# A recurrent layer times a routed expert layer: routed rows that carry their weight, and a new order of the units

## Chip, cores and metric

The kernel runs on one core of one Trainium2 chip. The metric is the device time of one execution in microseconds (us). Five engines work beside each other, each through its own queue in order: PE (matrix multiplies; PEld is its weight loads), DVE and ACT (elementwise work; ACT also evaluates the nonlinear functions), POOL (elementwise work, and it issues indirect DMAs) and SP (issues DMAs). They wait for one another by semaphores.

## What is computed

All data are float32: x is 4 x 1024 tokens of 256 channels. It is normalised (xn), and two branches are computed from xn:

```python
# branch 1: recurrence
xt = layernorm(xn) * ln_w + ln_b;  xp = xt shifted by one token
K, V = mix(xt, xp, mk) @ Wk.T, mix(xt, xp, mv) @ Wv.T
R = sigmoid(mix(xt, xp, mr) @ Wr.T)
S[t] = S[t-1] * decay + K[t]
s = xn + (R * (S * first + K) * V) @ Wo.T
# branch 2: experts, 8 of 128 hidden channels, the best 2 of the better group of 4
w = the two chosen sigmoid scores / their sum
f = sum over the 2 chosen e: w[e] * ((silu(xn @ w_gate[e]) * (xn @ w_up[e])) @ w_down[e])
f += (silu(xn @ sw_gate) * (xn @ sw_up)) @ sw_down      # shared expert
out = x + s * silu(f)
```

## The kernel before

**Groups.** The tokens are 8 groups g of 512 (two to a batch row b), each held as 4 tiles of 128 tokens. `norm` (moments on DVE, a square root on ACT at L311, a DVE product at L322) makes xn from x, `turn_xn` transposes it on PE, and ACT copies the result out. `norm2`, `norm2_out` and `turn_xt` do the same for the second norm. `diff` (POOL, L370) and `mix` (DVE, L645) make the mixed inputs. `gate` (L660), `recur` (L673 to L677), `value` (L682 on DVE, L683 on POOL) and `project_out` (L691 on PE, L694 on DVE, which overwrites xn) are the recurrence.

**Shared expert.** `shared_in` multiplies with the weights held on PE and 512 tokens moving, so that its result `hs` is already turned. `shared_out` multiplies down and ACT copies it to `acc` (L717).

**Routing.** `scores` computes router logits (64 small matmuls in all, L384) and their sigmoid (L388). `choose` picks the experts on DVE for a batch row, `place` computes each token's row in a list by expert and scatters it there with 16 indirect DMAs on POOL (L492); the list `xs` lies in DRAM. `plan`, once per half of the batch (two rows), starts with a matmul `cnt` (L506) and a DVE comparison `more` (L515), and derives which expert each tile of 128 list rows has; it ends with zero rows written behind each expert's list (L555).

**Expert tiles.** Each half has 39 tiles, worked on in 20 pairs: `tile_load` (SP, L589, three `xe` buffers), `tile_turn` (four transposes a pair, L597, copied by ACT, L599), `tile_in` (`gu`, L607, silu L611, product L612), `tile_back` (transposes L619, ACT copy L621), `tile_out` (`ye`, L628, ACT copy L630, then SP writes to `ys`, L632).

**Combining.** `fetch` gathers the two expert rows of 128 tokens with two indirect DMAs on POOL (L737), into six buffers. `combine` adds them on DVE, times their weights, to `acc` (L748). `final` applies silu on ACT (L757), multiplies by s and adds x on DVE (L758, L759) and writes out (SP, L760).

**Order.** The list ORDER (L25 to L117) is written out by hand or by a planner and holds every unit. PE, DVE and ACT execute in exactly this order; the chains of `follow` (L197) order the queues of SP and POOL. Tiles with a `bufs` count are recycled, so an instruction that writes such a tile waits for the last reader of the one before.

## Time and profile before

| What | Value |
|---|---|
| median of 8 runs | 417.92 us (413.98 to 420.27) |
| the profiled execution's own time | 421.44 us |
| its span (first to last instruction) | 419.7 us |
| busy PE / PEld / DVE / ACT / POOL | 345.1 / 241.3 / 253.7 / 195.0 / 171.3 us |
| mean granted clock of TensorE | 0.925 |
| 78 `xe` loads, 78 `ys` writes | 128 KB each |
| DMA | 58.96 MB, mean 140 GB/s |

A group line reads: line, engine, operation, output <- inputs, shape, count | busy us, mean ns of one | idle time of the engine just before, and what ended it. A line of a timeline reads: start us, duration us, engine, line, operation, output <- inputs, count [idle before <- what ended it]. A line of a table of stretches reads: from:to, its length, the busy time (and instructions) of PE, PEld, DVE, ACT and POOL, the granted clock, the DMA share and GB/s. Busy times of overlapping instructions are counted once in a total.

### The profile page before, as it was taken

Reading aid. Unit: us, or ns where it says so; the run is one execution under the profiler, and the core shown is the slowest. Engines: PE = TensorE matmul, PEld = TensorE weight load, DVE = VectorE, ACT = ScalarE, POOL = GpSimd, SP = SyncE. Lnnn points to the kernel's source line nnn. Section 1 sums busy time; section 2 is a strip of 40 time slices with the busy share of each in tenths; the row PEclk is TensorE's granted clock in tenths of the full one; section 3 lists DMA queues with packets and bytes.
Section 4 is the critical chain, followed back from the end, with each engine's and each line's share of the span. In section 5 each row is a group of like instructions: output and inputs, shape, how many; then the busy total and the mean of one; then the engine's idle time right before and its main releaser. Section 6 shows DMA issues by size and latency. Waiting matters only on the chain.

```text
span 419.7 us, 5291 instructions
## 1 busy us (share of the span) xinstructions
PE 345.1 (82%) x1426; PEld 241.3 (57%) x1426; DVE 253.7 (60%) x642; ACT 195.0 (46%) x347; POOL 171.3 (41%) x190
## 2 busy tenths in 40 slices
PE   1999957986899899539689998998679999977950
PEld 1756434662488687336248886787357856526430
DVE  4679984823934373434531544944348879689686
ACT  1874463453477654053156795153186443432501
POOL 7101576472010026727620131567610234768760
PEclk9999985989899899859969999999989999998986
DMA  7984141121544326215262564358655343516544
GB/s 223 308 266 145 55 152 44 52 100 50 164 138 149 104 79 215 109 60 167 100 210 67 184 181 125 99 162 231 197 159 177 106 142 108 152 37 187 150 124 139
DMA packets 52748, 58.96 MB, mean 140 GB/s; under 512 B 6800, under 2 KB 48272, under 8 KB 52720
## 3 DMA queue, kind: packets, MB, share of 16 engines
q1 hardware_dynamic: 45552, 40.39, 30.7%
q0 software_dynamic: 6608, 18.23, 13.4%
q8 instruction: 12, 0.20, 0.2%
q14 instruction: 16, 0.13, 0.1%
q10 hardware_dynamic: 560, 0.02, 0.1%
HBM read 31.61 MB, written 27.00 MB: 140 GB/s over the span
## 4 chain that ended last, share of the span: by engine, by line
PE 42%; DVE 19%; another core or an unknown queue 9%; DMA 8%; issue 8%; ACT 7%; SPq 3%; POOL 2%; ACTq 0%; DVEq 0%; POOLq 0%
PE gu L607 11%; PE ye L628 6%; PE r L653 5%; PE y L691 4%; DVE mix L645 3%; PE v L653 3%; PE tre L597 3%; PE k L653 3%; DVE acc L748 3%; DMA xe<-xs 2%; DVE S L673 2%; PE trh L619 2%; PE sh L703 2%; DMA got<-ys,back 2%
## 5 line engine op out<-in xcount | busy, mean ns | idle before, releaser
L492 POOL DMA_INDIRECT xs<-xn,idx x64 | 62.7, 980 | 43.0 <-DVE den L483 24.8
L737 POOL DMA_INDIRECT got<-ys,back x64 | 64.0, 999 | 39.3 <-issue 14.3
L607 PE MATMUL gu<-wgu,xeT 128*128 x312 | 75.5, 385 | 0.0
L607 PEld LDWEIGHTS gu<-wgu,xeT 128*128 128x128 f32 x312 | 58.1, 194 | 8.6 <-issue 1.7
L683 POOL TENSOR_TENSOR A<-A,rs 128x512 f32<-128x512 f32 x16 | 21.9, 1377 | 99.6 <-DVE A L682 96.5
L612 DVE TENSOR_TENSOR act<-act,gu 128x256 f32<-128x256 f32 (+1 forms) x40 | 16.5, 412 | 70.8 <-ACT act L611 64.1
L628 PE MATMUL ye<-wd,hT 128*128 x156 | 41.9, 394 | 0.0
L748 DVE SCALAR_TENSOR_TENSOR acc<-got,wt,acc 128x256 f32<-128x256 f32 x64 | 32.3, 512 | 13.9 <-DMA got<-ys,back 12.2
L645 DVE SCALAR_TENSOR_TENSOR mix<-d,vec,xtT 128x512 f32<-128x512 f32 x48 | 38.2, 842 | 0.0
L630 ACT COPY yes<-ye 128x512 f32<-128x512 f32 (+1 forms) x40 | 23.0, 577 | 32.7 <-PE ye L628 13.7
L370 POOL TENSOR_TENSOR d<-xtT 128x1024 f32<-128x1024 f32 x8 | 15.3, 1916 | 54.2 <-ACT xtT L362 25.6
L597 PE MATMUL tre<-ident,xe 128*128 128x128 f32 x156 | 26.0, 280 | 13.3 <-ACT hT L621 5.3
L691 PE MATMUL y<-wo,A 128*128 128x256 f32 x128 | 31.8, 398 | 4.5 <-POOL A L683 4.5
L703 PE MATMUL sh<-xnT,wgus 128*128 128x512 f32 x64 | 34.1, 688 | 0.0
L611 ACT ACTIVATE act<-gu 128x256 f32<-128x256 f32 (+1 forms) x40 | 15.2, 380 | 40.2 <-PE gu L607 22.3
L628 PEld LDWEIGHTS ye<-wd,hT 128*128 128x128 f32 x156 | 29.3, 200 | 5.5 <-issue 2.2
L653 PE MATMUL r<-mix,wr 128*128 128x512 f32 x64 | 31.3, 636 | 0.0
L597 PEld LDWEIGHTS tre<-ident,xe 128*128 128x128 f32 x156 | 19.2, 143 | 20.9 <-issue 7.7
L653 PE MATMUL k<-mix,wk 128*128 128x512 f32 x64 | 31.1, 614 | 0.0
L599 ACT COPY xeT<-tre 128x512 f32<-128x512 f32 (+1 forms) x40 | 23.0, 576 | 16.1 <-PE tre L597 8.7
L691 PEld LDWEIGHTS y<-wo,A 128*128 128x128 f32 x128 | 24.9, 201 | 9.5 <-POOL A L683 6.2
L653 PE MATMUL v<-mix,wv 128*128 128x512 f32 x64 | 29.7, 594 | 0.6 <-DVE A L677 0.6
(127 smaller groups left out, 536.8 us busy)
## 6 DMA issues: line engine op xcount, KB each, us to landing
xe<-xs SPq DMA_DIRECT2D x78, 128.0 KB
ys<-yes SPq DMA_DIRECT2D x78, 128.0 KB
xs<-zeros SPq DMA_DIRECT2D x32, 128.0 KB
xf<-in_x SPq DMA_DIRECT2D x16, 256.0 KB
out<-acc SPq DMA_DIRECT2D x16, 256.0 KB
xg<-in_x SPq DMA_DIRECT2D x7, 512.0 KB
wgu<-in_w_gate SPq DMA_DIRECT2D x8, 128.0 KB
wgu<-in_w_up SPq DMA_DIRECT2D x8, 128.0 KB
```

Of the source, the lines that this page charges most:

```text
L492: put = nc.gpsimd.indirect_dma_start(out=xs[h][:, :], out_offset=bass.IndirectOffsetOnAxis(ap=idx[:, k, n : n + 1], axis=0), in_=xn[:, n % ...
L597: nc.tensor.transpose(tr[:, c, j, :], p["xe"][:, j, ts(c, P)], ident)
L599: nc.scalar.copy(p["xeT"][:, :, :n], tr[:, :, :n])
L607: nc.tensor.matmul(gu[:, j, :], p["xeT"][:, c, j, :], wgu[:, e, c, :], start=(c == 0), stop=(c == CC - 1))
L628: nc.tensor.matmul(y[:, j, :], p["hT"][:, j, :], wd[:, e, :], start=True, stop=True)
L630: nc.scalar.copy(ye[:, :n], y[:, :n])
L645: nc.vector.scalar_tensor_tensor(m[:, c, :], d[:, c, :], vec[:, c, which : which + 1], xtT[:, c, 0:G], ALU.mult, ALU.add)
L653: nc.tensor.matmul(ps, w[:, c, ts(dc, P)], src[:, c, :], start=(c == 0), stop=(c == CC - 1))
L691: nc.tensor.matmul(ps[:, j, :], A[:, c, ts(2 * h + j, P)], wo[:, c, :], start=(c == 0), stop=(c == CC - 1))
L703: nc.tensor.matmul(p, wgu_s[:, c, ts(i, I)], xnT[:, c, :], start=(c == 0), stop=(c == CC - 1))
L737: follow(nc.gpsimd.indirect_dma_start(out=got[:, :], out_offset=None, in_=ys[b // BPH][:, :], in_offset=bass.IndirectOffsetOnAxis(ap=route ...
L748: nc.vector.scalar_tensor_tensor(acc, parts.pop((g, i, k)), route_of[b]["wt"][:, k, n : n + 1], acc, ALU.mult, ALU.add)
```

## The change

- x is loaded straight into the tile that keeps xn, and `norm` works in place; each token row there is 264 columns wide (W), 8 more than before. `norm` and `norm2` treat one, two or four groups at once.
- A routed row carries its weight in column 256. Since a token has two weights, ACT makes a second copy of its rows (`copy_rows`); POOL clears the extra columns. `place` writes the weights into the rows, and the scatters send 264 columns.
- `tile_out` scales its result by the weight while copying from PSUM, one ACT instruction per tile instead of one per pair; it reads the weight from `xe`. There are four `xe` buffers instead of three.
- `fetch` gathers with addition straight into `acc`, four tiles of one choice k at a time; `combine` is gone.
- The router's 8 columns are joined to the shared expert's weights. `shared_in` now holds 128 tokens and moves 264 weight columns; `scores` is gone, ACT copies the logits out and `choose` applies the sigmoid. `shared_turn` transposes the result.
- The gate uses tanh(z/2): `value` multiplies by (tanh + 1) and `project_out` by 0.5. A has two buffers.
- ORDER is new as a whole: more of the shared expert and all norms stand ahead of the expert tiles, and less is left behind them.

```diff
--- before.py
+++ after.py
@@ ORDER (whole list replaced; its beginning, the end of its tile stage and its end) @@
+    ("norm", 0, 1), ("turn_xn", 0, 0), ("turn_xn", 0, 1), ("norm2", 0, 1), ("norm2_out", 0), ("norm", 1, 1),
+    ("shared_in", 0, 0), ("load_x", 4), ("shared_in", 0, 1), ("turn_xn", 1, 0), ("turn_xn", 1, 1),
+    ("shared_turn", 0), ("turn_xt", 0, 0), ("turn_xt", 0, 1), ("shared_out", 0, 0), ("norm", 2, 2),
+    ("shared_in", 1, 0), ("load_x", 5), ("shared_in", 1, 1), ("turn_xn", 2, 0), ("load_x", 6), ("load_x", 7),
+    ("diff", 0), ("turn_xn", 2, 1), ("mix", 0, 2), ("choose", 0), ("shared_out", 0, 1), ("turn_xn", 3, 0),
+    ("shared_turn", 1), ("shared_in", 2, 0), ("turn_xn", 3, 1), ("shared_in", 2, 1), ("copy_rows", 1),
+    ("shared_out", 1, 0), ("copy_rows", 0), ("shared_out", 1, 1), ("place", 0), ("shared_turn", 2), ("gate", 0),
+    ("norm2", 1, 1), ("norm2_out", 1), ("shared_out", 2, 0), ("shared_out", 2, 1), ("turn_xt", 1, 0),
+    ("turn_xt", 1, 1), ("norm", 4, 4), ("shared_in", 3, 0), ("shared_in", 3, 1), ("turn_xn", 4, 0),
+    ("turn_xn", 4, 1), ("choose", 1), ("turn_xn", 5, 0), ("copy_rows", 3), ("turn_xn", 5, 1), ("copy_rows", 2),
+    ("shared_turn", 3), ("shared_in", 4, 0), ("shared_out", 3, 0), ("shared_in", 4, 1), ("shared_out", 3, 1),
+    ("place", 1), ("shared_turn", 4), ("turn_xn", 6, 0), ("plan", 0), ("shared_out", 4, 0), ("turn_xn", 6, 1),
...
+    ("tile_out", 1, 19), ("fetch", 4, 0), ("gate", 6), ("final", 1, 0), ("fetch", 4, 1), ("shared_out", 6, 0),
+    ("mix", 7, 2), ("project_out", 4, 0), ("final_load", 4, 1), ("fetch", 5, 0), ("project_out", 4, 1),
+    ("recur", 6, 0), ("final", 4, 0), ("shared_out", 6, 1), ("shared_turn", 7), ("final_load", 5, 0),
...
+    ("final_load", 6, 0), ("fetch", 7, 0), ("gate", 7), ("recur", 7, 0), ("recur", 7, 1), ("project_out", 6, 1),
+    ("value", 7, 1), ("final", 6, 1), ("value", 7, 0), ("project_out", 6, 0), ("final_load", 7, 0), ("final", 6, 0),
+    ("fetch", 7, 1), ("final_load", 7, 1), ("project_out", 7, 1), ("project_out", 7, 0), ("final", 7, 0),
+    ("final", 7, 1),
...
+    W = C + 8
...
-    xs = [dram.tile([NROW, C], F32, tag=f"xs{h}", name=f"xs{h}") for h in range(NH)]
+    xs = [dram.tile([NROW, W], F32, tag=f"xs{h}", name=f"xs{h}") for h in range(NH)]
...
-        xg = tok.tile([P, NT, C], F32, tag="xg", name=f"xg_{g}", bufs=3)
+        xg = keep.tile([P, NT, W], F32, tag=f"xn{g}", name=f"xn_{g}")
+        state[g]["row0"] = xg
+        xg = xg[:, :, 0:C]
...
+    wgu_s = wts.tile([P, CC, 2 * I + E], F32, tag="wgus", name="wgus")
...
+    nc.scalar.dma_start(wgu_s[:, :, 2 * I :], routerT.rearrange("(c p) e -> p c e", p=P))
...
+    def norm(g, many):
+
+        mv, rstd = moments(range(g, g + many), 1)
+        for n in range(many * NT):
+            xn = state[g + n // NT]["xn"][:, n % NT, :]
+            nc.vector.tensor_scalar(xn, xn, mv[:, n, 0:1], rstd[:, n : n + 1], ALU.subtract, ALU.mult)
+
+    def copy_rows(g):
+
+        row = tok.tile([P, NT, W], F32, tag="row1", name=f"row1_{g}", bufs=2)
+        for r in (row, state[g]["row0"]):
+            follow(nc.gpsimd.memset(r[:, :, C:], 0.0))
+        nc.scalar.copy(row[:, :, 0:C], state[g]["xn"])
+        state[g]["row1"] = row
+
+    def norm2(g, many):
+
+        n_all = many * NT
+        mv, rstd = moments(range(g, g + many), 2)
+        off = small.tile([P, 4 * NT], F32, tag="off", name=f"off_{g}", bufs=2)
+        nc.vector.scalar_tensor_tensor(off[:, :n_all], mv[:, :n_all, 0], -1.0, rstd[:, :n_all], ALU.mult, ALU.mult)
+        for i in range(many):
+            state[g + i]["norm2"] = off[:, ts(i, NT)], rstd[:, ts(i, NT)]
 
...
-    def scores(b, hb):
-        if hb == 0:
-            scores_of[b] = small.tile([P, BT, E], F32, tag="sc", name=f"sc_{b}", bufs=2)
-        xnT = state[b * GPB + hb]["xnT"]
-        lg = ps_tr.tile([P, G], F32, tag="tr", name=f"lg_{b}_{hb}")
-        for n in range(NT):
-            for c in range(CC):
-                nc.tensor.matmul(
-                    lg[:, ts(n, E)], xnT[:, c, ts(n, P)], rw[:, c, :], start=(c == 0), stop=(c == CC - 1)
-                )
-        sc = scores_of[b][:, ts(hb, NT), :]
-        nc.scalar.activation(sc.rearrange("p n e -> p (n e)"), lg[:, : NT * E], AF.Sigmoid)
-
     def choose(b):
 
         sc = scores_of[b]
+        flat = sc.rearrange("p n e -> p (n e)")
+        nc.scalar.activation(flat, flat, AF.Sigmoid)
 
...
-        wt = keep.tile([P, K, BT], F32, tag=f"wt{b}", name=f"wt_{b}")
-        tt(wt, w, den.unsqueeze(1).to_broadcast([P, K, BT]), ALU.mult)
-        route_of[b].update(wt=wt, row=got[:, 0, :])
+        for i in range(GPB):
+            for k in range(K):
+                tt(state[b * GPB + i][f"row{k}"][:, :, C], w[:, k, ts(i, NT)], den[:, ts(i, NT)], ALU.mult)
+        route_of[b].update(row=got[:, 0, :])
 
         for n in range(BT):
-            xn = state[b * GPB + n // NT]["xn"]
             for k in range(K):
                 put = nc.gpsimd.indirect_dma_start(
                     out=xs[h][:, :], out_offset=bass.IndirectOffsetOnAxis(ap=idx[:, k, n : n + 1], axis=0),
-                    in_=xn[:, n % NT, :], in_offset=None,
+                    in_=state[b * GPB + n // NT][f"row{k}"][:, n % NT, :], in_offset=None,
                 )
...
-        xe = exp.tile([P, 2, C], F32, tag="xe", name=f"xe_{h}_{u}", bufs=3)
+        xe = exp.tile([P, 2, W], F32, tag="xe", name=f"xe_{h}_{u}", bufs=4)
...
-        nc.scalar.copy(ye[:, :n], y[:, :n])
+        for j in range(n):
+            nc.scalar.activation(ye[:, j, :], y[:, j, :], AF.Copy, scale=p["xe"][:, j, C : C + 1])
...
-            nc.scalar.activation(r[:, dc, :], ps[dc], AF.Sigmoid)
+            nc.scalar.activation(r[:, dc, :], ps[dc], AF.Tanh, scale=0.5)
...
-            st["A"] = chan.tile([P, CC, G], F32, tag="A", name=f"A_{g}", bufs=1)
+            st["A"] = chan.tile([P, CC, G], F32, tag="A", name=f"A_{g}", bufs=2)
...
-        tt(A, A, v_ps, ALU.mult)
-        follow(nc.gpsimd.tensor_tensor(A, A, state[g]["r"][:, dc, :], ALU.mult))
+        rv = state[g]["r"][:, dc, :]
+        nc.vector.scalar_tensor_tensor(rv, rv, 1.0, v_ps, ALU.add, ALU.mult)
+        follow(nc.gpsimd.tensor_tensor(A, A, rv, ALU.mult))
 
...
-        tt(xn[:, 2 * h : 2 * h + 2, :], ps, xn[:, 2 * h : 2 * h + 2, :], ALU.add)
-
-
-    def shared_in(g):
-        xnT = state[g]["xnT"]
-        ps = []
-        for i in range(2):
-            p = ps_mm.tile([P, G], F32, tag="mm", name=f"sh{i}_{g}")
+        half = xn[:, 2 * h : 2 * h + 2, :]
+        nc.vector.scalar_tensor_tensor(half, ps, 0.5, half, ALU.mult, ALU.add)
+
+
+    def shared_in(g, half):
+
+        b, hb = divmod(g, GPB)
+        st = state[g]
+        if half == 0:
+            st["hs"] = ffn.tile([P, NT, I], F32, tag="hs", name=f"hs_{g}", bufs=1)
+            if hb == 0:
+                scores_of[b] = small.tile([P, BT, E], F32, tag="sc", name=f"sc_{b}", bufs=2)
+        for n in range(2 * half, 2 * half + 2):
+            ps = ps_mm.tile([P, 2 * I + E], F32, tag="mm", name=f"sh_{g}_{n}")
             for c in range(CC):
-                nc.tensor.matmul(p, wgu_s[:, c, ts(i, I)], xnT[:, c, :], start=(c == 0), stop=(c == CC - 1))
-            ps.append(p)
-        hs = ffn.tile([P, G], F32, tag="hs", name=f"hs_{g}")
-        nc.scalar.activation(hs, ps[0], AF.Silu)
-        tt(hs, hs, ps[1], ALU.mult)
-        state[g]["hs"] = hs
+                nc.tensor.matmul(ps, st["xnT"][:, c, ts(n, P)], wgu_s[:, c, :], start=(c == 0), stop=(c == CC - 1))
+            h = st["hs"][:, n, :]
+            nc.scalar.activation(h, ps[:, 0:I], AF.Silu)
+            nc.scalar.copy(scores_of[b][:, hb * NT + n, :], ps[:, 2 * I :])
+            tt(h, h, ps[:, I : 2 * I], ALU.mult)
+
+    def shared_turn(g):
+        tr = ps_tr.tile([P, G], F32, tag="tr", name=f"trs_{g}")
+        for n in range(NT):
+            nc.tensor.transpose(tr[:, ts(n, P)], state[g]["hs"][:, n, :], ident)
+        state[g]["hsT"] = ffn.tile([P, G], F32, tag="hsT", name=f"hsT_{g}", bufs=1)
+        nc.scalar.copy(state[g]["hsT"], tr)
 
     def shared_out(g, half):
-        hs = state[g]["hs"]
+        hs = state[g]["hsT"]
...
-    parts = {}
-
-    def fetch(g, i):
+    def fetch(g, k):
 
         b, hb = divmod(g, GPB)
-        n = hb * NT + i
-        for k in range(K):
-            got = exp.tile([P, C], F32, tag="got", name=f"got_{g}_{i}_{k}", bufs=6)
+        for i in range(NT):
+            n = hb * NT + i
             follow(nc.gpsimd.indirect_dma_start(
-                out=got[:, :], out_offset=None, in_=ys[b // BPH][:, :],
+                out=state[g]["acc"][:, i, :], out_offset=None, in_=ys[b // BPH][:, :],
                 in_offset=bass.IndirectOffsetOnAxis(ap=route_of[b]["back"][:, k, n : n + 1], axis=0),
+                compute_op=ALU.add, oob_is_err=True,
             ))
-            parts[g, i, k] = got
-
-    def combine(g, i):
-        b, hb = divmod(g, GPB)
-        n = hb * NT + i
-        acc = state[g]["acc"][:, i, :]
-        for k in range(K):
-            nc.vector.scalar_tensor_tensor(
-                acc, parts.pop((g, i, k)), route_of[b]["wt"][:, k, n : n + 1], acc, ALU.mult, ALU.add
-            )
 
```

## The prediction, on record before the run

> **What bounds the kernel now.** I read the busy shares first, then the stretches of the span, the chain of work that ended last, and the timeline where two stretches meet.
>
> ```profile
> PE 345.1 (82%) x1426; PEld 241.3 (57%) x1426; DVE 253.7 (60%) x642; ACT 195.0 (46%) x347; POOL 171.3 (41%) x190
> ...
> PE 42%; DVE 19%; another core or an unknown queue 9%; DMA 8%; issue 8%; ACT 7%; SPq 3%; POOL 2%; ACTq 0%; DVEq 0%; POOLq 0%
> ```
> PE is busiest, but it holds only 42% of the chain, so the stages differ. The busy times by stretch (PE, PEld, DVE, ACT, POOL) show how:
>
> ```profile
> 0.00:113.60 113.60, 89.20 (x327) 55.46 (x327) 76.62 (x256) 56.68 (x90) 47.35 (x75) 0.91 0.42 141
> 113.60:275.00 161.40, 137.95 (x664) 107.43 (x665) 75.36 (x222) 83.75 (x158) 52.70 (x50) 0.93 0.42 133
> 275.00:350.20 75.20, 67.89 (x288) 48.99 (x289) 46.46 (x80) 33.01 (x69) 29.46 (x27) 0.98 0.55 165
> 350.20:419.70 69.50, 50.03 (x151) 29.37 (x149) 55.22 (x87) 21.61 (x31) 41.82 (x39) 0.89 0.43 131
> ```
> I cut at the first transpose of an expert tile (113.6) and the last expert matmul (350.2). The **tile stage** between is PE's: 205.8 busy in 236.6 us, 30.8 idle. **Head** and **tail** are not: PE idles 24.4 and 19.5 us there.
>
> The head ends when the first tile is loaded, behind 32 row scatters on POOL (first at 45.32, second batch 78.14 to 98.3) and the plan of the tiles:
>
> ```profile
> 97.30 0.97 POOL L492 DMA_INDIRECT xs<-xn,idx  x1 [0.30 <-issue]
> 98.35 0.19 PEld L703 LDWEIGHTS sh<-xnT,wgus 128*128 128x128 f32 x1 [0.24 <-issue]
> 100.91 0.20 ACT L388 ACTIVATE sc<-lg 128x32 f32<-128x32 f32 x1 [9.30 <-remote]
> 100.96 0.29 DVE L515 TENSOR_TENSOR more<-cnt,steps 128x128 f32<-128x128 f32 x1 [6.48 <-remote]
> ```
> The plan's first instruction (`more`) needs a matmul recorded at 90.34 to 90.71, yet starts at 100.96, when the 16 shared-expert matmul records queued after it have drained. From `more` to the first transpose are 12.6 us.
>
> The tail is POOL's queue of 32 gathers, then the last groups' outputs:
>
> ```profile
> 354.38 0.98 POOL L737 DMA_INDIRECT got<-ys,back  x1 [2.14 <-DMA ys<-yes]
> ...
> 407.09 0.99 POOL L737 DMA_INDIRECT got<-ys,back  x1 [0.30 <-issue]
> ...
> 415.54 0.69 DVE L759 TENSOR_TENSOR acc<-acc,xf 128x512 f32<-128x512 f32 x1
> ```
> One gather takes 0.96 and the next comes 0.30 later, 1.26 each. POOL runs 53.7 us from 354.4 to 408.1; 11.6 us later the span ends.
>
> **Base.** The profiled execution took 421.44 us (span 419.7, 1.7 around it); the median of the runs is 417.92. I work out differences on the profiled one and take them off the median.
>
> **Engine by engine.** Prices are from the groups and the timeline.
>
> ```profile
> L748 DVE SCALAR_TENSOR_TENSOR acc<-got,wt,acc 128x256 f32<-128x256 f32 x64 | 32.3, 512 | 13.9 <-DMA got<-ys,back 12.2
> L384 PE MATMUL lg<-rw,xnT 128*128 128x8 f32 x128 | 18.7, 278 | 3.3 <-ACT xnT L342 2.0 <-issue 1.3
> L311 ACT ACT_TABLE_LOAD x11 | 14.1, 1283 | 6.6 <-DVE mv L310 6.4
> L660 ACT ACT_TABLE_LOAD x6 | 7.7, 1283 | 12.8 <-PE r L653 12.7
> ```
> *PE.* The router's own matmuls go: 16 records take 1.85 at 161.66, eight units, -14.8. The shared expert changes from 32 matmuls of 512 columns (8 records in 3.43, 27.4 in all) to 64 of 264; a 256-column `gu` pair takes 0.43, so 264 take 0.445, 28.5 in all, +1.1. Turning its result adds 8 x 4 transposes (four take 0.60), +4.8. Net -8.9.
>
> *DVE.* Combining goes, -32.3. `hs` is cut in 32 products of 128 columns (0.29, from the 128x128 `act` row) for 8 of 0.68, +3.8. Batched norms save about -2. The weight columns, value and project_out forms add about +3. Net -28. Half of the combining lay in the tile stage beside PE, where it costs nothing; in the tail DVE is the busiest, 55 of 69.5.
>
> *ACT.* The new instruction list has 22 table loads for 41, by stage 14/8/0 for 17/19/5: -24.4. Against it: scaled tile output, 78 of 128x256 at 0.39 for 40 at 0.58, +7.4; shared silu and logit copies, 32 x (0.28 + 0.20) for 6.2, +9.2; eight row copies of 1024 columns, twice the 512-column copy's 0.58 less its start, about 1.05, +8.4; eight `hsT` copies, +4.6. Net about +5: ACT isn't relieved, only its loads leave the path from PE to PE.
> On the loads the timeline has one at 82.48 for 1.28 and its ACTIVATE at 83.77, nothing between. The Trainium skill (ScalarE: Activation LUTs, What ACT_TABLE_LOAD costs) puts a drain of 1.38 us beside each load; by it the 19 loads would be about 50 us of ACT (an estimate) instead of 24.4. The row shows no such gap, and the sum goes by the row.
>
> *POOL.* As many scatters and gathers, plus 16 memsets (128x8 takes 0.10): +1.6.
>
> *Rows.* They grow from 1024 to 1056 bytes, +3% on transfers at a DMA share of 0.42. The page DMA: Bandwidth & Descriptors (How a descriptor splits into AXI transactions) speaks against the new length: a row that doesn't start 256-byte aligned takes extra beats, by an estimate 36.5 for 32. That would be about 0.27 us on an `xe` landing of 1.95, where the length alone gives 0.06; no run here shows it.
>
> **Stage by stage** (units in the new order times these prices).
>
> *Head.* PE work falls from 73.8 to 67.2 and DVE's is 84 for 86, so what counts is POOL's start. Following DVE: norm 0 ends at 9.7 as now, second norm 12.5, norm 1 16.6, shared products about 20, norms 2 and 3 (8.1 and a table load) 28.5, shared 1 and mix 31, choose(0) 6.9, shared 2, place 2.9: first scatter about 42.5 for 45.3. Then norm2(1), the four norms at once (15), shared 3, choose(1), shared 4, place(1): 75, ending at 95.5 for 98.3. The plan now stands right behind place(1) with few matmuls queued after `cnt`; it should be done at about 83 and its zeros landed by 90. The load then waits for the scatters alone: 95.5 + 2 landing + 2 load, and gate(1), placed ahead, needs a difference that POOL makes after the scatters. First transpose about 102.5: **-11**. Ends: 0 if `cnt` is late again, -15.
>
> *Tile stage.* PE work goes from 206.4 to 211.3, +4.9. Eleven loads fewer give at most -14; I take -7, as some stood beside PE. With as much other idling that is about -2. **A new wait** comes against it. A tile's `xe` now holds the weights too, so it's free after tile_out's scaling, not after tile_turn; there are four buffers for three. Counted in PE work, from the release to the tile_turn that needs the refill, the old order leaves 7 to 25 us (most over 9), the new one under 5.5 in 14 of 36 cases. A refill needs 0.78 (two scaled copies), 0.9 (two issues) and 1.95 landing, 3.6. With two `ys` writes ahead in SP's queue (0.9) and one ACT copy ahead (0.5) it is 5.0; summed over the places with less, the shortage is 6. I take **+5**; bounds 0 (lead 3.6) and 27 (lead 6.5). Behind a waiting `xe` issue on SP stand `ys`, `out` and `xf` transfers. Stage: +3 to +4.
>
> *Tail.* PE 38.4 for 45.0, DVE 33.5 for 53.9, no loads; POOL 32 x 1.26 + 4 products x 1.26 = 45.4. From the last expert matmul to the first gather 4.2 stay. No gather waits for a buffer that DVE frees, but each second gather of a token tile waits until the first has landed, four gathers (5.0 us) earlier; a plain one lands 2.6 to 4.2 after its issue. After the last: landing 2.6, silu 0.63, two products 1.4, write and end 3.5, some waits 1.5, in all 9.6. 4.2 + 45.4 + 1.3 + 9.6 = 60.5 for 69.5: **-9**. An add in the gather appears in no row. Below: nothing extra (a gain is excluded: it moves the same bytes and reads more). Above: POOL at twice 0.95, +30. Nearest is the plain gather, whose issue and 128 rows are the same, so I add 0 and keep 30.
>
> Other edits are priced at nothing: two buffers for A, norms in place, x loaded ahead, the tanh form; if the cover of the four-group norm on DVE fails, 15 us move into the head.
>
> Sum: -11 + 4 - 9 = **-16**: 405.4 for the profiled execution, 402 beside the median.
>
> **Rivals.**
> *Refills set the tile stage (slower).* For: the short distances; SP already waited 48.7 us for tile outputs. Against: today PE waits only 5.0 us for `xe`. With a lead of 6.5 instead of 5.0 the shortage is 27, 22 over mine: 424. It decides from about 6.1.
> *The added gather is dear.* For: it must read its target too, and pairs depend on each other. Landing in 8 us makes four second batches wait 3 each: 414. POOL at double price: 432.
> *The head doesn't move*, since `cnt` or the four-group norm comes late: 413.
> *More comes than forecast:* refills are hidden (-5) and a quarter of the tile stage's idle goes (-8): 389.
> *The change doesn't do what it says:* excluded for the combining, router matmuls and loads, which are gone from the list.
>
> **Chances.** Forecast 402 (own range 393 to 409) 0.42; more 389, 0.17; gather late 414, 0.14; head 413, 0.07; refills 424, 0.15; POOL double 432, 0.05. Half a per cent, about what can be told from no change, is 415.8 to 420. About 0.06 of the 413 and 414 cases fall there: faster 0.74, same 0.06, slower 0.20. Range 384 to 425: it leaves out the double price and what lies under 389.
>
> **What would show it.** Right: first transpose at 100 to 105; last expert matmul 236 to 242 later; POOL's last gather at most 53 after that; 22 loads. Wrong: PE idle before `tre` by `xe` over 12 us in all; a gather on POOL over 1.3 us or landing after more than 5; `more` waiting after place(1).

## The result and the profile after

The change made the kernel slower: a median of 440.56 us (10 runs, 438.21 to 445.29) where the kernel before takes 419.45 (29 runs), a ratio of 1.0549 with a 95% interval of 1.0506 to 1.0592. Forecast was 402, range 384 to 425. The profiled execution took 439.8 us, its span is 438.0. The profiled executions of the kernel before and, below, of tail_plain_2, after_again and before_pace03 ran 1.6 to 1.8% longer than the fastest runs of their kernels, so differences of stages read from them hold to a few microseconds only.

The busy times by stretch after the change, cut at the first transpose of an expert tile and at the last expert matmul as before:

```profile
0.00:112.70 112.70, 76.80 (x315) 55.06 (x316) 75.67 (x282) 65.05 (x144) 46.82 (x82) 0.88 0.49 156
112.70:359.80 247.10, 213.81 (x948) 159.46 (x947) 113.03 (x273) 118.77 (x262) 104.47 (x87) 0.94 0.50 135
359.80:438.00 78.20, 47.12 (x134) 29.05 (x132) 34.18 (x50) 11.53 (x21) 60.33 (x38) 0.80 0.58 113
```

| | before | forecast | after | missed by |
|---|---|---|---|---|
| head | 113.6 | 102.6 | 112.7 | 10.1 |
| tile stage | 236.7 | 240.2 | 247.1 | 6.9 |
| tail | 69.4 | 60.4 | 78.2 | 17.8 |
| span | 419.7 | 403.2 | 438.0 | 34.8 |

All three steps failed, and all in one direction. The table's last column is what the experiments have to explain. PE is 12.4 us less busy in the head (6.6 were forecast from the list of units), but idle for 35.9 us there instead of 24.4. The granted clock doesn't explain the loss: in the tile stage it is 0.94 before and after, and in the tail, where it fell from 0.89 to 0.80, the chain that ended last lies on POOL and not on PE. The costliest groups show the rest:

```profile
L737 POOL DMA_INDIRECT acc<-ys,back x64 | 102.3, 1598 | 22.4 <-issue 18.0
...
L682 PE MATMUL y<-wo,A 128*128 128x256 f32 x128 | 39.4, 464 | 21.9 <-POOL A L674 16.0
...
L585 PE MATMUL tre<-ident,xe 128*128 128x128 f32 x156 | 25.6, 279 | 12.5 <-DMA xe<-xs 9.9
```
A gather that adds holds POOL for 1.6 us where a plain one held it 1.0 (64 of them, 102.3 us for 64.0); products of the recurrence, which are queued behind gathers on POOL, now keep PE waiting (all 16.0 us of it in the tail); and PE waits for `xe` more than before.

### The profile page after: what moved, and what is told of

Read it like the earlier page. It is cut to its first block, busy times and chain, and to the rows that moved or that the text cites. A ratio compares the mean times of both kernels' runs of the same rounds, so it can differ in the third digit from the quotient of the medians.

```text
span 438.0 us, 5353 instructions
## 1 busy us (share of the span) xinstructions
PE 337.7 (77%) x1394; PEld 243.6 (56%) x1394; DVE 222.9 (51%) x604; ACT 195.3 (45%) x427; POOL 211.6 (48%) x206
## 4 chain that ended last, share of the span: by engine, by line
PE 37%; POOL 18%; issue 12%; ACT 8%; DVE 8%; DMA 6%; another core or an unknown queue 6%; SPq 2%; POOLq 1%; ACTq 0%; DVEq 0%
POOL acc L737 18%; PE gu L595 8%; PE sh L700 5%; PE ye L616 4%; PE v L642 3%; PE k L642 3%; DMA xe<-xs 3%; PE y L682 3%; PE tre L585 2%; PE r L642 2%; DMA acc<-ys,back 2%; DVE st L302 2%; PE dn L719 2%; ACT yes L619 1%
## 5 line engine op out<-in xcount | busy, mean ns | idle before, releaser
L737 POOL DMA_INDIRECT acc<-ys,back x64 | 102.3, 1598 | 22.4 <-issue 18.0
L674 POOL TENSOR_TENSOR A<-A,rs 128x512 f32<-128x512 f32 x16 | 23.5, 1556 | 99.1 <-DVE rs L673 99.1
L682 PE MATMUL y<-wo,A 128*128 128x256 f32 x128 | 39.4, 464 | 21.9 <-POOL A L674 16.0
L480 POOL DMA_INDIRECT xs<-xn,idx x32 | 31.3, 978 | 45.9 <-DVE xn L475 23.7
L682 PEld LDWEIGHTS y<-wo,A 128*128 128x128 f32 x128 | 29.4, 237 | 29.7 <-POOL A L674 17.9
L619 ACT ACTIVATE yes<-ye,xe 128x256 f32<-128x256 f32 x78 | 32.8, 474 | 12.0 <-PE ye L616 7.8
L480 POOL DMA_INDIRECT xs<-row,idx x32 | 31.7, 992 | 9.7 <-issue 8.5
L700 PE MATMUL sh<-wgus,xnT 128*128 128x264 f32 x128 | 34.0, 416 | 2.4 <-issue 1.5
L748 ACT ACTIVATE acc<-acc 128x512 f32<-128x512 f32 x16 | 10.0, 630 | 52.5 <-DMA acc<-ys,back 52.5
L700 PEld LDWEIGHTS sh<-wgus,xnT 128*128 128x128 f32 x128 | 26.0, 210 | 8.0 <-issue 2.4
```

Source lines behind the costliest of these rows:

```text
L480: put = nc.gpsimd.indirect_dma_start(out=xs[h][:, :], out_offset=bass.IndirectOffsetOnAxis(ap=idx[:, k, n : n + 1], axis=0), in_=state[b * ...
L619: nc.scalar.activation(ye[:, j, :], y[:, j, :], AF.Copy, scale=p["xe"][:, j, C : C + 1])
L674: follow(nc.gpsimd.tensor_tensor(A, A, rv, ALU.mult))
L682: nc.tensor.matmul(ps[:, j, :], A[:, c, ts(2 * h + j, P)], wo[:, c, :], start=(c == 0), stop=(c == CC - 1))
L700: nc.tensor.matmul(ps, st["xnT"][:, c, ts(n, P)], wgu_s[:, c, :], start=(c == 0), stop=(c == CC - 1))
L737: follow(nc.gpsimd.indirect_dma_start(out=state[g]["acc"][:, i, :], out_offset=None, in_=ys[b // BPH][:, :], in_offset=bass.IndirectOffset ...
```

## The experiments

**Theory** after the first look: the add in the gather pays for the tail, the longer hold of `xe` for the tile stage, and results of PE that reach ACT late for the head. **Rivals**: the tail follows landing and PE, not POOL; loads of 1056-byte rows are slow in themselves; the change only stirs up what the kernel before suffers too.

The experiments ran on four chips, and these turned out to be of two kinds. On two of them the kernel before takes 418 to 420 us, on the two others 385. I call them **late** and **clear** chips, for a reason that comes out below. A time is only compared with the kernel before on its own chip. Which chip gave the result above isn't on record; with 419.45 us for the kernel before it looks like a late one.

### Plain gathers everywhere (late chip)

```
- out=acc[:, i, :], ..., compute_op=ALU.add
+ out=got[:, i, :], ...                     # 2 buffers of 4 token tiles
+ tt(acc, acc, got, ALU.add)                # DVE, ahead of the next but one fetch
```


> The changed kernel with plain gathers into two buffers of four token tiles, which DVE then adds to acc (1024 columns at once, 16 additions); the rows still carry their weights and everything else is as changed. Theory: the add in the gather is what the tail pays for. A gather falls from 1.56 + 0.30 to 0.97 + 0.30 on POOL, 32 of them in the tail give 19 us back, and the products on POOL that stood behind the gathers of the first half a few more (the 6.5 us wait of PE for them): 440.6 becomes 415 to 421, the tail 58 to 60 us. Rival: the tail follows PE and the landing of the gathers, and POOL only looks full: then DVE's additions and the wait for a free buffer cancel the gain, 433 to 445, with POOL idle between the gathers.

Measured: 442.63 us, ratio 1.0576 (1.0492 to 1.0660). No gain, which is the rival's number, but not for the rival's reason. The last expert matmul came at 370.6 instead of 359.8; from there to the end are 69.5 us instead of 78.2. The tail gave back 8.7, the tile stage lost 9.5 and the head 1.3. POOL's waits in the tile stage of this kernel (engine, tile, line, what it waited for: us in total, times, longest):

```profile
POOL got L739 <- DVE acc L746: 19.6, 2, 16.9
```
DVE runs in the order of the list, where I had put an addition too late, and POOL stood for its buffer, 16.9 us at one place. The run couldn't part the price of the add from the price of what replaced it.

### xe released early (late chip)

```
+ nc.scalar.copy(p["w"][:, :n], p["xe"][:, :n, C])    # behind the copy of xeT
- nc.scalar.activation(ye[:, j, :], ..., scale=p["xe"][:, j, C : C + 1])
+ nc.scalar.activation(ye[:, j, :], ..., scale=p["w"][:, j : j + 1])
  ORDER: 32 of 40 tile_load right behind the tile_turn that frees their buffer
```


> The changed kernel, but ACT copies the two weights of a pair out of xe right behind the copy of its transposes (40 small copies more), so that xe is free from then on; 32 of the 40 loads are issued right behind the tile_turn that frees their buffer. Theory: the waits before tre for xe (16.9 us against 5.0 before) come from the buffer held to tile_out; they fall to 3 to 7 us, and the time by 5 to 11, to 430 to 436, less 0 to 3 us that the small copies cost on ACT. Rival: the load itself is slow, because rows of 1056 bytes land later than rows of 1024 or because SP's queue stands behind ys writes: the waits stay above 12 us and the time within 437 to 443.

Measured: 436.0 us, ratio 1.0423 (1.0337 to 1.0510), 4.6 less than the change. PE's waits before `tre` for `xe` are gone altogether, with rows as long as before, so their cause was when the buffer came free and was asked for again, and not the row length. They were 9.9 us in the changed kernel and 2.5 in the one before; the 16.9 and 5.0 of the expectation add the waits of PE's weight loads (PEld), which are much the same waits seen a second time. But PE's idle time in the tile stage stayed, 33.6 us for 33.3. And the unedited change takes 436.36 us on another late chip (below), so a gain in time isn't shown. The timeline of this kernel (start, duration, engine, line, operation; idle before and what ended it) shows what took the place of the waits:

```profile
308.79 0.63 ACT L749 ACTIVATE acc<-acc 128x512 f32<-128x512 f32 x1 [13.11 <-DMA acc<-ys,back]
309.32 0.35 ACT L610 COPY hT<-trh 128x256 f32<-128x256 f32 x1
...
309.73 1.11 PE L584 MATMUL tre<-ident,xe 128*128 128x128 f32 x4 [10.89 <-ACT hT L610]
```
ACT stands 13.1 us at the silu of a `final`, in its fixed order, for gathers of the first half that POOL hasn't got through yet; behind it waits the copy that PE needs. The dear gathers reach into the tile stage: 32 of them take POOL from 258 to 322 here.

### rates first (late chip)

`ORDER` with `("rates",)` at the front, out of the way of the second norm of group 2.

> The changed kernel with the unit rates (two table loads and two small activations, 96.71 to 99.71 on ACT) moved to the front of the list. Theory: in the head the second norm of group 2 stands behind it on ACT and PE waits for that (9.42 us before trt), so the first transpose of an expert tile comes 3 us earlier, near 109.7, and the time falls by 1 to 3 us, to 437.5 to 439.5. Rival: the head is set by PE's late results (acc<-dn at 96.12, ten us after its matmuls) or by the scatters, and something else takes the place of the two loads: first transpose within 1 us of 112.7, time within 1 us of 440.6.

Measured: 439.81 us, ratio 1.0518 (1.0400 to 1.0637); first transpose at 111.0 for 112.7. The 1.7 us in the head agree with the sign but are no more than heads with the same order differ by here (112.4 to 114.3); the time doesn't decide either: its interval holds both expectations.

### A stream of products beside five kinds of work

The head of the changed kernel shows what set it. On ACT, a copy starts at 96.12 whose matmuls are recorded at 84.02 to 86.01, and the releaser is unknown ("remote": the profile shows nothing that ended the wait); the loads for `rates` and the second norm follow, and PE waits for that:

```profile
84.02 1.99 PE L719 MATMUL dn<-wds,hsT 128*128 128x256 f32 x8 [2.26 <-issue]
...
96.12 0.58 ACT L720 COPY acc<-dn 128x512 f32<-128x512 f32 x1 [4.62 <-remote]
...
102.45 2.80 PE L335 MATMUL trt<-ident,xt 128*128 128x128 f32 x8 [9.42 <-ACT xt L347]
...
112.66 1.04 PE L585 MATMUL tre<-ident,xe 128*128 128x128 f32 x8
```
The tiles themselves were asked for at 95.40. Such late copies fall into bursts of scatters in both kernels; a kernel of its own was to say why.

> A kernel of its own, which leaves out the whole computation but a stream of products: a product of 512 columns (two matmuls in the list) into PSUM, copied out by ACT and DVE in turn, in stretches of 20 products with one kind of work beside each and 8 products with none between: 24 indirect scatters of 128 rows of 1024 bytes, 24 direct writes of as many bytes from SP, 24 plain gathers, 24 gathers that add, 24 products on POOL. Theory: results of PE come late only while POOL issues indirect DMAs (in both kernels the copies behind PE start 4 to 10 us after the recorded end of their matmuls in those stretches and under 0.5 elsewhere): the copies lag by over 2 us, or the products take longer than 1.75 us each, beside scatters and gathers alone. Rival: the bytes do it, then the direct writes show it too; or POOL's traffic does, then the products on POOL show it. Second question: the price of the add by itself, 0.97 and 1.56 us a gather as in the two kernels, or less when no gather waits for another.

Measured (274.2 us, a late chip): ACT's copies come every 3.43 us, except late in the two bursts of plain indirect DMAs. ACT's timeline beside the scatters (issued 24.5 to 55) and beside gathers that add:

```profile
40.24 0.59 ACT L141 COPY scatter<-ps 128x512 f32<-128x512 f32 x1 [2.85 <-PE ps L135]
44.39 0.59 ACT L141 COPY scatter<-ps 128x512 f32<-128x512 f32 x1 [3.56 <-PE ps L135]
54.95 0.59 ACT L141 COPY scatter<-ps 128x512 f32<-128x512 f32 x1 [9.97 <-issue]
58.54 1.07 ACT L141 COPY scatter<-ps 128x512 f32<-128x512 f32 x2 [3.00 <-PE ps L135]
...
183.28 0.59 ACT L141 COPY gather_add<-ps 128x512 f32<-128x512 f32 x1 [2.85 <-PE ps L135]
186.71 0.59 ACT L141 COPY gather_add<-ps 128x512 f32<-128x512 f32 x1 [2.85 <-PE ps L135]
```
After 13 scatters a copy is still in time (40.24), after 16 one is 0.7 late (44.39), and the next, due at 47, comes at 55, while PE's records go on to 57.57. Plain gathers do the same (a gap of 12.79). Direct writes of as many bytes, products on POOL, and gathers that add do nothing. So neither the bytes nor a busy POOL are enough. The add's price stands by itself too: 1.54 us on POOL against 0.95 plain, with no gather waiting for another.

### The same pieces on a clear chip

Four kernels fell on a chip where the kernel before takes 385.13 us.

> The changed kernel; only the gathers of the second half (groups 4 to 7, the 32 of the tail) are plain, into two buffers that DVE adds to acc; the first half still adds in the gather. It parts what the plain gathers gave in the tail from what the additions on DVE cost in the tile stage, where the run with plain gathers everywhere lost 9 us (POOL waited 16.95 us there for an addition that stood late in DVE's order). Theory: the tail falls from 77.5 to about 69, as in that run, the tile stage stays at 247.5, the time is 430 to 434. Rival: what was lost in the tile stage there was not the additions but the plain gathers themselves, which crowd PE's results, and in the tail the same happens: then the whole gain is under 4 us, 437 to 441.

> Three edits together on the changed kernel: plain gathers everywhere with the addition on DVE placed ten units behind its gather in the list (no longer as late as the next buffer allows), xe released by a copy of its weights with the loads issued earlier, and rates at the front. Theory: the early release alone gave 4.6 us and not 10, because ACT then stood 13.1 us at a silu of final for gathers that add and were not through; with faster gathers that wait goes too. Tail -8.5, xe waits -15, rates -1, a part of it lost again to late results beside plain gathers (6 us): 418 to 427, close to the kernel before. Rival: the additions on DVE hold up the tile stage wherever they stand: 432 to 440.

> The changed kernel with a memset of 128x640 (about 0.6 us on POOL) behind each scatter of batch rows 2 and 3, so that they come 1.9 us apart instead of 1.27, and each batch row takes 30 us instead of 20. The list of the second half is read at 247, 16 us after the last scatter, so the longer bursts should hide. Theory: results of PE come late when some 13 or more indirect DMAs are issued 1.27 us apart and not when they are 1.86 apart; the idle time of PE in the two bursts (9.7 us in 166 to 196 and 9.1 in 205 to 240) falls to under 6 in all and the time by 6 to 12, to 429 to 435. Rival: the late results come from the scattered writes as such or from other work: the idle time stays, and products on POOL behind the longer bursts come later: 439 to 446.

> The stream of products alone again (the rest of the computation is left out), beside five kinds of indirect scatters: 16 in a row, 24 with a pause of 0.3 us behind each, 18 with 0.6, 24 in three lots of 8 with 5 us between, and 24 of half the rows (64 of 1024 bytes). Theory: what counts is how many are issued back to back, since with 24 the first 12 or 13 did nothing and then the copies stood for 10 us, and gathers that add, 1.86 us apart, did nothing at all: 16 in a row hold the copies for 2 to 5 us, lots of 8 and the pause of 0.6 not at all, the pause of 0.3 little. With half the rows the issue is shorter if it goes by rows, and then it shows whether the limit counts DMAs (held after 13) or rows (held after 26, so not at all). Rival: it is the time that POOL is busy, whatever it issues: then the pauses on POOL change nothing, and the copies are held in all but the lots of 8.

The edits: `fetch` is plain for groups 4 to 7 alone (tail_plain); plain gathers with the addition ten units behind, `xe` released early and rates first (plain_release); a POOL memset of 0.6 us behind scatters (paced). In paced the memsets didn't stand where I meant them: those of batch row 2 ran in one block ahead of its scatters, and six of row 3's too.

Measured: tail_plain 389.04 us, 1.0105 (1.0060 to 1.0149); plain_release 383.23, 0.9896 (0.9851 to 0.9941), 1% faster than before; paced 407.4, 1.0553 (1.0503 to 1.0603). In lag2 every copy comes every 3.43 us, beside 16 scatters in a row too, and in none of these four profiles does a wait end in an unknown releaser, though the three whole kernels keep bursts of 16 scatters 1.27 us apart. That answered nothing on what in a burst does it, but it shows that the late results go with the chip. (The 24 scatters in a row that held the copies never ran on a clear chip.) The head of tail_plain, which is the changed kernel's own, on this chip:

```profile
82.61 0.33 PE L335 MATMUL trt<-ident,xt 128*128 128x128 f32 x1 [0.29 <-ACT xt L347]
...
93.86 1.04 PE L585 MATMUL tre<-ident,xe 128*128 128x128 f32 x8
```
The transposes that waited until 102.45 start at 82.61, and the first expert tile at 93.9.

### Both kernels again, and the stream (a second late chip)

> The changed kernel once more, unedited, beside the kernel before. The last four runs were on another chip, on which the kernel before takes 385.1 us instead of 420.4, no wait ends in an unknown releaser in any kernel, and the stream of products is never held. Theory: some chips bring PE's results late beside bursts of indirect DMAs, others don't, and both kernels lose about the same by it, so that the change costs the same on both: +19 to +22 us, 404 to 407 where before takes 385, and 440 where it takes 420. Rival: the changed kernel only does badly because of the late results, since its gathers that add suffer none and its head and scatters more: then it is within 2% of before, 378 to 393, on a chip without them.

> The kernel before, unedited, for its trace on this chip. Theory: on a chip that takes 385 us for it, the first transpose of an expert tile comes near 95 to 100 instead of 113.6 (the comparison in plan waits no longer ten us for its matmul), the tile stage takes 215 to 222 instead of 236.6, and the tail 66 to 70; waits for an unknown releaser are gone. Rival: it isn't late results but a higher clock or faster transfers; then all stages shrink alike, by 8%, and single instructions are shorter.

> The stream of products beside five kinds of work (the rest of the computation left out) as it ran first, on a chip where the kernel before took 420 us; there the copies were held for some 10 us beside 24 plain scatters and 24 plain gathers, and not beside gathers that add. Theory: it goes with the chip: where before takes 385 us the copies come every 3.43 us throughout; where it takes 420 they are held again in the same two stretches. Rival: it is chance, or it needs more than 16 scatters in a row (the second kernel of this kind had 24 only with pauses or of half the rows): then they are held here too.

> The changed kernel with a memset of about 0.6 us behind each scatter of batch rows 2 and 3. On the chip without late results it took 407.4 us against 385.1 for before, where nothing could be gained by it; how the unedited change does there decides whether it cost something. Theory: on a chip without late results within 3 us of the unedited change, a little more rather than less (the products behind the bursts come later); on a chip with them 6 to 12 us less than the unedited change. Rival: it costs 5 us and more on either.

This chip was a late one, so what the expectations say of a clear chip stayed untested. Measured: the change 436.36 us, ratio 1.0429 (1.0336 to 1.0522), 17 us more for the 19 to 22 expected; its stages are 107.8, 253.4 and 78.1. Before takes 417.84, stages 113.7, 233.4 and 69.0. So the head gains 5.9 us here, where it gained 0.9 in the first trace, and the tail loses 9.1. The stream is held in the same two stretches again and no others (gaps of 11.34 beside scatters, 12.71 beside plain gathers), so it wasn't chance. The same paced kernel, 407.4 on the clear chip, takes 427.04 here, 1.0249 (1.0137 to 1.0360): 9.3 us less than the unedited change, all in the tile stage (heads and tails agree within 0.3). Since its memsets stood wrongly, that needed another run.

### Add, pace, and all causes together (late chip)

> The changed kernel with plain gathers for groups 4 to 7 alone, once more, for a chip where before takes 420 us. On the other chip it was 1.0105 times before, where the change with paced scatters, which keeps the gathers that add, was 1.0553: 17 us apart. Theory: the add is what the tail pays for, and 32 of them cost 19 us on POOL; late results beside plain gathers take some of it back here: tail 66 to 70 instead of 77.5, time 426 to 434 (1.02 to 1.035 times before). Rival: beside plain gathers PE's results come so late that the gain is lost: tail 74 to 78, time over 436.

> The changed kernel with a memset of 128x640 on POOL behind each scatter of batch rows 2 and 3, now in that order for certain: 16 scatters in 30 us. Theory: at 1.9 us apart no result of PE is late; the idle time of PE in and just behind the two bursts is under 5 us in all, where the unedited change has some 19, and the time is 425 to 431 where the change takes 436 to 440. On a chip where before takes 385 it gains nothing, 402 to 410. Rival: the first paced kernel gained by what its order changed besides (one burst 10 us later) and the pace does nothing: 434 to 442.

> The changed kernel with what the runs so far blame taken away: plain gathers with the addition on DVE ten units behind, xe released early with earlier loads, rates first, and the scatters of batch rows 2 and 3 paced. Without the pace it was 0.99 times before on the chip without late results. Theory: the causes add up: tail -8, xe -5, late results -9 from 438: 408 to 420, 0.975 to 1.0 times before. Rival: the plain gathers bring late results of their own to the tile stage, as in the run with plain gathers everywhere, where the tile stage grew by 9 us: 420 to 430.

> The kernel before with two memsets of 128x256 on POOL (some 0.6 us) behind each scatter of batch row 2 alone; row 3 stays as it is, since the second half reads the list 3 us after its last scatter. Theory: the 11.6 us that PE is idle in that burst and just behind it fall to 3 or less, but the scatters of row 3 come at least as late as now: 411 to 416, 0.98 to 0.99 times before. Rival: the burst ends 10 us later, row 3 with it, and the second half waits for its list: 420 to 428.

```
  follow(put, loose=True)
+ if b in (2, 3):                              # before_paced: b == 2, two of 128x256
+     follow(nc.gpsimd.memset(pace, 0.0))      # 128x640
```

*tail_plain_2*: ratio 1.0231 (1.0121 to 1.0340), from runs of 428.5 and 429.8 us; from the last expert matmul (362.5) to the end 71.9 us for 78.2. On the clear chips the tail is 70.9 with plain gathers and 78.2 with gathers that add (paced). So taking the add away gives the tail 6 to 7 us net on either kind, of 19.2 on POOL. In tail_plain_2 the rest is lost again in three places: POOL waits 7.4 for the addition that frees a buffer and 2.0 for the input of a product, and behind the last gather the end comes 3.6 later than after the change, since an addition stands there too:

```profile
386.14 0.95 POOL L741 DMA_INDIRECT got<-ys,back  x1 [0.30 <-issue]
394.45 0.94 POOL L741 DMA_INDIRECT got<-ys,back  x1 [7.37 <-DVE acc L748]
```

*paced_strict*: 428.49 us, 1.0229 (1.0141 to 1.0317), some 8 to 12 less than the change. The waits of PE over a microsecond in and behind the two bursts, first the unedited change (after_again), then the paced kernel:

```profile
191.14 2.08 PE L616 MATMUL ye<-wd,hT 128*128 x4 [10.47 <-ACT hT L609]
219.77 0.69 PE L607 MATMUL trh<-ident,act 128*128 128x128 f32 x2 [2.27 <-issue]
225.42 0.44 PE L607 MATMUL trh<-ident,act 128*128 128x128 f32 x2 [1.04 <-issue]
227.13 0.39 PE L494 MATMUL cnt<-upto,ones 128*128 128x8 f32 x2 [1.27 <-issue]
232.38 2.08 PE L616 MATMUL ye<-wd,hT 128*128 x4 [4.86 <-DVE xn L686]
```
```profile
205.38 0.66 PE L610 MATMUL trh<-ident,act 128*128 128x128 f32 x2 [4.29 <-DVE act L603]
237.40 0.99 PE L588 MATMUL tre<-ident,xe 128*128 128x128 f32 x4 [3.64 <-DMA xe<-xs]
```
19.9 us become 4.3 and a wait of 3.6 for the list, which is now later. From 165 to 245 us, around the two bursts, the waits that end in an unknown releaser are these, first in after_again, then in the first paced kernel (paced_again), where the burst of row 2 ran without pauses:

```profile
DVE S L663 <- remote: 7.7, 1, 7.7
DVE xn L686 <- remote: 6.3, 1, 6.3
ACT yes L619 <- remote: 4.6, 1, 4.6
ACT hT L609 <- remote: 2.7, 1, 2.7
```
```profile
DVE S L666 <- remote: 5.5, 1, 5.5
ACT act L602 <- remote: 4.6, 1, 4.6
```
Both of the latter lie beside row 2. Beside row 3, where nine scatters of sixteen were paced, there is none, and in paced_strict there is none beside either burst. Late results of PE go with scatters 1.27 us apart, and not with scatters 1.8 us apart.

*plain_release_paced*: 418.75 us, 0.9976 (0.9933 to 1.0019): the change so edited is level with the kernel before, on a late chip. Not every late result is gone from it: the first half's plain gathers run without pauses, beside them PE waits 5.7, 2.2 and 7.6 us, and the tile stage takes 238.3 us where plain_release took 216.0 on the clear chip. *before_paced*: 413.02 us, 0.9859 (0.9776 to 0.9941), faster than both kernels, by a pause alone. It stops where the next wait stands, a product on POOL behind both bursts:

```profile
208.61 4.14 PE L695 MATMUL y<-wo,A 128*128 128x256 f32 x8 [15.24 <-POOL A L687]
```

### How much of a pause (clear chip)

> The stream of products alone (the rest of the computation is left out) beside 16 indirect scatters in a row, 24 with a pause of 0.3 us behind each, 18 with 0.6, 24 in three lots of 8 with 5 us between, and 24 of half the rows (64 of 1024 bytes). Where before takes 385 us all copies came every 3.43 us. Theory, for a chip where before takes 420: a backlog of scatters builds up that is through after 12 to 13 in a row; so 16 in a row hold the copies for 1 to 5 us, pauses of 0.6 and lots of 8 not at all, half the rows not at all if the backlog is of rows or bytes. Rival: it is the number issued, whatever the pace: then the 24 with a pause of 0.3 and the 18 with 0.6 hold the copies as the 24 without did. A third case: the chip shows none again, then it stays open.

> The kernel before with one memset of 128x256 (0.3 us on POOL) behind each scatter of batch rows 2 and 3. Theory: a pause of 0.3 brings the rate from one in 1.27 to one in 1.7 us, close to the 1.86 of the gathers that add, at which nothing was late: PE idles under 8 us beside the two bursts instead of 18.5, while the bursts end only 7 us later each and the product on POOL is less late: 407 to 413, 0.97 to 0.985 times before. Rival: 0.3 is too little, or the second half waits 7 us for its list: 414 to 422.

Both fell on the second clear chip (before 385.26), so neither expectation was tested. lag2_again shows no held copy. before_pace03, one memset of 0.3 us behind each scatter of rows 2 and 3, has a ratio of 1.0114 (1.0019 to 1.0208); its four runs spread from 386.8 to 395.0 us, so it gains nothing where nothing is late, and how much it costs is open. Its head is that of the kernel before and ends at 104.0. What in a burst makes results late (number, rate or rows) stays open.

## Why the prediction was wrong

**Head, -11 forecast, -0.9 measured.** The scatters moved as worked out and better: first at 36.47 (42.5 forecast), second batch at 73.12 (75), through at 93.9 (95.5); the plan didn't wait for `cnt` and the loads went out at 95.40. What failed is the last sentence of the step, "First transpose about 102.5". The second norm of group 2 and `gate(1)`, ahead of it in the list, hang on ACT, and ACT stood until 96.12 for a result of PE that was late beside the second burst, then took two loads for `rates`. On the clear chips, without the late results, the step nearly holds: 93.9 to 97.6 for kernels with the change's head and 104.0 for before's, 6 to 10 us less. On the second late chip it gained 5.9. I had seen the late `cnt` of the kernel before and carried it only as an end of the range for the same instruction; the burst was still there, so another one stood in its place.

**Tile stage, +3 to +4 forecast, +10.4 measured.** Three terms of the sum were mis-sized, each by 2 to 3 us. PE's work was forecast +4.9 and is +7.9. The new wait for `xe` was forecast +5; PE's waits for it before `tre` rose by 7.4 us (us in total, times, longest; before and after):

```profile
PE tre L597 <- DMA xe<-xs: 2.5, 2, 1.5
PE tre L585 <- DMA xe<-xs: 9.9, 13, 2.1
```
PE's other idle time, which the eleven loads fewer (22 in all, as counted) were to cut by 7, fell by 4.9. Together that is +10.4. The prediction's "today PE waits only 5.0 us for `xe`" adds PE's 2.5 and the 2.5 of its weight loads, and its sign of being wrong, 12 us, is passed only in that count (16.9). Undoing the hold took these waits away but no idle time in sum: it uncovered the next wait, the gathers of the first half, which no step of mine had in the tile stage. Why PE's work grew by 3 us more than counted is open; with the same tiles it is 209.8 us in early_release and 217.0 in rates_first. The traces of the second late chip give 233.4 and 253.4 for the stage, so the terms hold to a few microseconds only. The late results are no visible part of the difference: beside the two bursts PE is idle 18.7 of 54 us before and 19.8 after.

**Tail, -9 forecast, +8.7 measured.** "An add in the gather appears in no row ... I add 0 and keep 30." It takes 1.56 us plus 0.30 where a plain one takes 0.96 plus 0.30; 32 of them in the tail are 19.2 us, and the step missed by 17.8. The rest of the sum fits: the first gather comes 4.3 us behind the last expert matmul (4.2 forecast), the end 7.8 behind the last gather (9.6), and in between POOL runs for 66.1 us back to back (46.7). No gather waited for another: only POOL's own time grew. The reason for 0, same rows and same issue, left out that POOL is held longer for the add itself. DVE fell from 55 to 34 us in the tail as forecast. The prediction calls the old tail POOL's queue; but in the chain that ended last it was more DVE's, with 13.5% of the tail for the combining (L748) and 5.5% for gathers. After the change the gathers are 52.8% of it. So the change took work from the engine that mostly set the end, and with the add made another one set it.

**Rivals.** "POOL at double price" had the mechanism, with a chance of 0.05; two thirds of the 30 us that it named came; "refills set the tile stage" and "the head doesn't move" came true in part. I treated them as alternatives, each over a forecast that was otherwise right, so that the range ended at 425. But the three stages follow one another, and their misses add up: 10.1 + 6.9 + 17.8 over 403.2 is the span of 438.0.

**Not shown:** the unedited change on a clear chip. From tail_plain there (389.04) and the two tails (70.9 and 78.2) I estimate 396, a ratio of 1.03: slower too, by less. Nor is it shown that the edits price the tail's add in full: they gave back 6 to 9 us of it, and the 19.2 is read from POOL's own rows.

## What to carry to other kernels

Work that is folded into an indirect DMA isn't free because its engine-side instruction is gone: look at which engine issues it and whether that engine sets the end, and price an unseen form from above when it sits on the bounding queue. The wait that the old kernel showed at one instruction belonged to the burst beside it, and came again at another; keep such a wait in the sum wherever the burst goes. Count an engine's wait once: a view that adds PE and its weight loads doubles it. Rivals that touch different stages can all come true, so the range has to hold their sum, not only each.

## What the runs showed of the hardware

- A gather that adds to its target took 1.54 us on POOL, a plain one 0.95 (24 each, 128 rows of 1024 bytes).
- On two chips results of PE reached ACT and DVE late beside plain indirect DMAs issued 1.27 us apart (in the stream by 8 to 10 us after some 16 of them), while PE's own records ran on; with scatters 1.8 us apart, adding gathers, direct writes or POOL products they didn't. On two other chips no wait ended in an unknown releaser. The same kernel before took 418 to 420 us on the first two and 385 on the others.
- A pause of some 0.6 us behind each scatter of one batch row gained 1.4% for the kernel before on a late chip (0.9859); a shorter one on two rows gained nothing on a clear chip (1.0114, 1.0019 to 1.0208).
- The late results as such were measured. Whether PE itself ran behind its records or only its results were passed on late, and whether the count, the rate or the rows decide, is open.
